# Moving three steps at the starts of two layers: a weight load to another queue, a pinned division, later denominators

## The chip, the cores and the metric

The kernel runs on one core of a Trainium2 chip. A core has a matrix engine (TensorE, PE in the profile), a vector engine (VectorE, DVE), an activation engine (ScalarE, ACT), a general engine (GpSimd, POOL) and a sync engine (SyncE, SP). They run side by side and wait for each other through semaphores. In this kernel SP and POOL also issue most of the transfers between the chip's main memory and the on-chip memory; each of them issues in its own order. The metric is the time of one execution on the device, in microseconds (us).

## The reference

Four graph layers in sequence on 3327 nodes with 512 features. Every layer adds its result to its input and normalises each row:

```python
x = _layernorm(x + _L0_gnn_ref(x, adj, L0_gnn_W, L0_gnn_a), axis=-1)
x = _layernorm(x + _L1_gnn_ref(x, adj, L1_gnn_W_nb, L1_gnn_b_nb, L1_gnn_W_line, L1_gnn_b_line, 64), axis=-1)
x = _layernorm(x + _L2_gnn_ref(x, adj, L2_gnn_W, L2_gnn_a), axis=-1)
x = _layernorm(x + _L3_gnn_ref(x, adj, L3_gnn_W, L3_gnn_a), axis=-1)
```

Layers 0, 2 and 3 are attention over the neighbours, with 8, 8 and 4 heads; layers 2 and 3 apply ELU to the result. For one head of layer 3:

```python
e = si[:, :, None] + sj[:, None, :]
e = jnp.where(e > 0, e, ALPHA * e)
e = jnp.where(adj[None, :, :] > 0, e, NEG_INF)
attn = jax.nn.softmax(e, axis=-1)
h_prime = jnp.einsum('hij,hjd->hid', attn, h)
```

Layer 1 takes the mean of a node's first 64 neighbours (in index order) and two linear maps:

```python
keep = Ab & (jnp.cumsum(Ab.astype(jnp.int32), axis=1) <= neibor_num)
nb_mean = (keep.astype(X.dtype) @ X) / jnp.maximum(cnt, 1.0)
xj = leaky_relu(nb_mean @ W_nb.T + b_nb)
xi = leaky_relu(X @ W_line.T + b_line)
return xi + jnp.where(cnt > 0, xj, 0)
```

## The kernel before

The rows are cut into NT = 26 tiles of 128 rows, and these into two halves of HALF = 13 tiles. Tiles are counted from 0, so the "fifth tile" is tile 4.

An attention layer first projects all tiles, then forms the attention of each half in four strips of columns. What a strip yields is still to be divided by the softmax's denominator: numerators go through tiles called hb to a tensor hd in main memory, and the denominators are collected on chip in rec. For the last strip of the second half they take a way round: they are summed on DVE to a tile red (line 505), stored to a tensor dd (line 507) and loaded back, rearranged, by 16 small transfers to a tile pes (place, lines 510 to 520). finish_sums (lines 525 to 538) then turns pes into the reciprocals in rec, by four DVE operations (lines 532 and 536) and a reciprocal (line 538). In layers 0 and 2 both steps of the last strip are put in a list, self.late, and done by the layer that follows. Only tiles 13 to 25 need them.

The next layer starts by finishing the rows of the last one, in pairs of tiles. finish_steps (line 165) gives a list of steps: load brings the numerators (h from hd, line 126) and the layer's input (xr, line 126); divide(s) multiplies the tile by rec on DVE (line 181) and, for ELU, has ACT take the exponential to a tile e (line 186); add(s) adds the input on DVE (line 197, or lines 194 and 195 with ELU); norm_rows takes the statistics (lines 152 and 153), a square root on ACT (line 154), a reciprocal and a product on DVE (lines 155 and 158), and normalises on ACT (line 161). The exponential and the square root lie in different tables of ACT, and the table is loaded again whenever it changes.

PE's instructions run in the order in which the program emits them. The instructions of the other engines and queues are put in order by a scheduler, except that keep_in_program_order pins an instruction behind everything that was emitted before it on its engine.

Layer 1 is sage (line 686). It loads two weights wn and wl (lines 716 and 717, through load_w, 1 MB each) and a bias on POOL. Then a loop goes over pairs of tiles. For each tile PE transposes it (pt, line 724), ACT copies it back (xT, line 726), and one tile later PE applies both weights (pz, line 732; pi, line 735) and DVE and ACT finish (lines 736 to 746). During the first tile of a pair the next pair is finished. At t0 = 4 the loop takes place from the late list, at t0 = 8 finish_sums.

Layer 3 starts in third (line 892). The loop is alike: PE transposes a tile (pt, line 261), ACT copies it (xT, line 262), DVE sums it (line 263), and one tile later PE projects it (pw, line 271), ACT and DVE scale the result (lines 272 to 277: dc, rc, qc, vt) and SP stores vt. load_group issues the loads of a pair three pairs ahead, with ten h buffers; the rest of a pair's steps is emitted during the first tile of the pair before it. After tile 14's transpose and tile 13's projection the loop prepares the attention of the first half (prepare, lines 298 to 322; PE's part is pr, line 312, and ACT's copy line 314). In finish_steps the argument pinned pins the exponential of a pair's first tile on ACT; it is set for the pair that begins with tile 2. Here too place is called at t0 = 4 and finish_sums at t0 = 8.

Of the kernel before, what the change touches and what calls it, by code (L numbers as in the profile page):

```python
# [32 lines left out]
def kernel(  # L33
# [10 lines left out]
    nc = tc.nc  # L44
# [90 lines left out]
    def load_w(pool, src, name, eng=None):  # L135
        t = pool.tile([P, FC, src.shape[1]], F32, name=name)
        (eng or nc.scalar).dma_start(out=t, in_=src.rearrange("(c p) m -> p c m", p=P))
        return t
# [26 lines left out]
    def finish_steps(pool, xin, layer, t0, n, hbufs=6, eng=nc.sync, xbufs=None, xpool=None, ebufs=None, pinned=False):  # L165
        H, D = layer.H, layer.D
        ys, xs, steps = [], [], []

        def load():
            for t in range(t0, t0 + n):  # L170
                h = pool.tile([P, F], F32, name="h", bufs=hbufs)
                load_tile(h, hd, t, eng)
                ys.append(h)
                xr = xpool.tile([P, F], F32, name="xr", tag="hb") if xpool else \
                    pool.tile([P, F], F32, name="xr", bufs=xbufs)
                load_tile(xr, xin, t, nc.gpsimd)
                xs.append(xr)

        def divide(s):
            h = ys[s]  # L180
            nc.vector.tensor_tensor(h.rearrange("p (h d) -> p h d", h=H), h.rearrange("p (h d) -> p h d", h=H),
                                    rec[:, t0 + s, :H].rearrange("p (h e) -> p h e", e=1).to_broadcast([P, H, D]),
                                    op=ALU.mult)
            if layer.elu:
                e = pool.tile([P, F], F32, name="e", bufs=ebufs)
                ins = nc.scalar.activation(e, h, AF.Exp)
                if pinned and s == 0:
                    tc.keep_in_program_order(ins)
                xs.append(e)

        def add(s):
            h, xr = ys[s], xs[s]
            if layer.elu:
                nc.vector.scalar_tensor_tensor(xr, xs[n + s], 1.0, xr, op0=ALU.min, op1=ALU.add)
                nc.vector.scalar_tensor_tensor(h, h, 0.0, xr, op0=ALU.max, op1=ALU.add)
            else:
                nc.vector.tensor_tensor(h, h, xr, op=ALU.add)

        steps.append(load)
        for s in range(n):  # L200
            steps += [lambda s=s: divide(s), lambda s=s: add(s)]
        steps.append(lambda: norm_rows(pool, ys, t0))
        return ys, steps

    def finish(*a):
        ys, steps = finish_steps(*a)
        for f in steps:
            f()
        return ys
# [476 lines left out]
    def sage(first, first_pool, xin, prev, nxt, wsrc, dst):  # L686
# [3 lines left out]
        with tc.tile_pool(name="sg_z", bufs=1, reuse_waits="tile") as zp, \  # L690
# [17 lines left out]
            def zs(t, c):  # L708
                return zs_[t // HALF][:, t % HALF, c, :]

            zd = dram.tile([NP, F], BF, name="zd")
            with tc.tile_pool(name="sa_w", bufs=1, reuse_waits="tile") as wp, \
                    tc.tile_pool(name="sa", bufs=2, reuse_waits="tile") as fp, \
                    tc.tile_pool(name="sa_t", bufs=2, reuse_waits="tile") as sp, \
                    tc.tile_pool(name="sa_ps", bufs=2, space=PSUM, reuse_waits="tile") as ps:
                wn = load_w(wp, wnT, "wn", nc.gpsimd)
                wl = load_w(wp, wlT, "wl", nc.gpsimd)
                blb = wp.tile([P, F], F32, name="blb")
                nc.gpsimd.dma_start(out=blb, in_=bl.to_broadcast([P, F]))

                def step1(xt):
                    pt = ps.tile([P, FC, P], F32, name="pt")
                    for c in range(FC):
                        nc.tensor.transpose(pt[:, c, :], xt[:, c * P:(c + 1) * P], ident)  # L724
                    xT = sp.tile([P, FC, P], F32, name="xT")
                    nc.scalar.copy(xT, pt)  # L726
                    return xT

                def step2(xt, xT, t):
                    pz = ps.tile([P, F], F32, name="pz")  # L730
                    for c in range(FC):
                        nc.tensor.matmul(pz, xT[:, c, :], wn[:, c, :], start=c == 0, stop=c == FC - 1)  # L732
                    pi = ps.tile([P, F], F32, name="pi")
                    for c in range(FC):
                        nc.tensor.matmul(pi, xT[:, c, :], wl[:, c, :], start=c == 0, stop=c == FC - 1)  # L735
                    nc.scalar.copy(zs(t, 0), pz)
                    r1 = sp.tile([P, F], F32, name="r1")
                    nc.vector.tensor_tensor(r1, pz, zs(t, 0), op=ALU.subtract)
                    nc.scalar.copy(zs(t, 1), r1)
                    z3 = sp.tile([P, F], BF, name="z3")  # L740
                    nc.vector.tensor_tensor(z3, r1, zs(t, 1), op=ALU.subtract)
                    nc.sync.dma_start(out=zd[t * P:(t + 1) * P, :], in_=z3)
                    xi = sp.tile([P, F], F32, name="xi")
                    nc.vector.tensor_tensor(xi, pi, blb, op=ALU.add)
                    nc.vector.scalar_tensor_tensor(xi, xi, 0.01, xi, op0=ALU.mult, op1=ALU.max)
                    nc.vector.tensor_tensor(xi, xi, xt, op=ALU.add)
                    nc.sync.dma_start(out=xid[t * P:(t + 1) * P, :], in_=xi)


                cr = fp.tile([NT, P], BF, name="cr", bufs=1)  # L750
                nc.sync.dma_start(out=cr, in_=ctd[NT:NT + 1, :].rearrange("o (t p) -> (o t) p", p=P))
                cnt = zp.tile([P, 3, NT], F32, name="cnt")
                pend = None
                ahead = first
                for t0 in range(0, NT, 2):
                    ys = ahead
                    if t0 in (4, 8):
                        prev.late.pop(0)(fp)
                    if t0 == 8:
                        cf = fp.tile([NT, P], F32, name="cf", bufs=1)  # L760
                        nc.scalar.copy(cf, cr)
                        pt = ps.tile([P, FC, P], F32, name="pt")
                        cb = pt[:, 0, :NT]
                        nc.tensor.transpose(cb, cf, ident[:NT, :NT])
                        nc.vector.tensor_scalar(cnt[:, 0, :], cb, NEIGHBOURS, 1.0, op0=ALU.min, op1=ALU.max)
                        nc.vector.reciprocal(cnt[:, 1, :], cnt[:, 0, :])
                        nc.vector.tensor_scalar(cnt[:, 2, :], cb, 0.0, None, op0=ALU.is_gt)
                    for s, y in enumerate(ys):
                        xT = step1(y)
                        if s == 0 and t0 + 2 < NT:  # L770
                            ahead = finish(fp, xin, prev, t0 + 2, 2, 6, nc.sync if t0 else nc.gpsimd)
                        if pend:
                            step2(*pend)
                        pend = (y, xT, t0 + s)
                step2(*pend)
            first_pool.close()

            with tc.tile_pool(name="sb_w", bufs=1, reuse_waits="tile") as wp, \
# [69 lines left out]
                for b in range(len(blocks)):  # L848
                    t0, i0 = blocks[b]
# [42 lines left out]
    def third(first):  # L892
        with tc.tile_pool(name="col3", bufs=1) as cp, tc.tile_pool(name="at_r3", bufs=2, reuse_waits="tile") as rp:
# [3 lines left out]
            with tc.tile_pool(name="p_w", bufs=1, reuse_waits="tile") as wp, \  # L897
# [13 lines left out]
                def load_group(t0):  # L911
                    if t0 < NT:
                        groups.append(finish_steps(fp, x2, L2, t0, 2, 10, nc.gpsimd if t0 < 4 else nc.sync, 6,
                                                    pinned=t0 == 2))
                        groups[-1][1].pop(0)()

                load_group(2)
# [2 lines left out]
                load_group(4)  # L920
                for t0 in range(0, NT, 2):
                    ys = ahead
                    if t0 in (4, 8):
                        L2.late.pop(0)(fp)
                    load_group(t0 + 6)
                    for s, y in enumerate(ys):
                        t = t0 + s
                        store_tile(x3, y, t, nc.sync)
                        xT = L3.project1(pp, ps, y, t)
                        if s == 0 and groups:  # L930
                            ahead, steps = groups.pop(0)
                            for f in steps:
                                f()
                        if pend:
                            L3.project2(pp, bank, wsb, *pend)
                        pend = (xT, t)
                        if t == HALF + 1:
                            L3.prepare(pp, 0)
                            L3.first_rows = L3.rows(rp, 0, 0)
                            L3.cut(pp, 0)  # L940
# [284 lines left out]
```

## Time and profile before

| | |
|---|---|
| time, median of 3 runs | 3389.97 us (3388.6 to 3393.65) |
| the profiled execution's own time | 3389.15 us |
| its span in the trace | 3387.4 us |
| mean granted clock of PE | 0.985 |
| PE busy | 3251.2 us, 96% of the span |
| DVE busy | 2687.5 us, 79% |
| ACT busy | 2354.6 us, 70% |
| POOL busy | 239.8 us, 7% |
| layer 1 starts (first transposes of sage) | near 958 us of the span |
| layer 3 starts (first transposes of third) | near 2556 us of the span |

Times inside the trace are us from the start of the span. A row of the timeline has the start, the length, the engine, the line, the operation, the tile written <- the tiles read with their shapes, the number of instructions in a row, and in brackets the idle time of the engine before it and what ended it. A row of the chain of waits has the start, the length and what the time went to: an engine with tile and line, a transfer (DMA), or "issue", time in which nothing that the profile shows was waited for. A row of the windows has the stretch, its length, the busy time of PE, PE's weight loads, DVE, ACT and POOL with their number of instructions, PE's granted clock, the busy share of the DMA engines, and GB/s.

### The profile page before, as it was taken

Reading aid. Unit: us, or ns where it says so; the run is one execution under the profiler, and the core shown is the slowest. Engines: PE = TensorE matmul, PEld = TensorE weight load, DVE = VectorE, ACT = ScalarE, POOL = GpSimd, SP = SyncE. Lnnn points to the kernel's source line nnn. Section 1 sums busy time; section 2 is a strip of 40 time slices with the busy share of each in tenths; the row PEclk is TensorE's granted clock in tenths of the full one; section 3 lists DMA queues with packets and bytes.
Section 4 is the critical chain, followed back from the end, with each engine's and each line's share of the span. In section 5 each row is a group of like instructions: output and inputs, shape, how many; then the busy total and the mean of one; then the engine's idle time right before and its main releaser. Section 6 shows DMA issues by size and latency. Waiting matters only on the chain.

```text
span 3387.4 us, 47182 instructions
## 1 busy us (share of the span) xinstructions
PE 3251.2 (96%) x18476; PEld 1626.4 (48%) x18476; DVE 2687.5 (79%) x2619; ACT 2354.6 (70%) x2143; POOL 239.8 (7%) x389
## 2 busy tenths in 40 slices
PE   8899999999979999999989999999998999999997
PEld 7634344444434445545544444444446754455453
DVE  5799999999967544444449999999998766668887
ACT  2398998999953333333338999999997655558986
POOL 3100000000010011111110000000002000010110
PEclk9999999999999999999999999999998999999998
DMA  9644111110143343333320111111117411122211
GB/s 368 222 124 127 49 49 38 55 49 28 44 123 125 122 117 84 91 85 87 80 77 20 47 48 50 51 48 47 35 31 241 152 41 42 41 51 80 94 42 49
DMA packets 288014, 284.29 MB, mean 84 GB/s; under 512 B 107492, under 2 KB 223534, under 8 KB 287791
## 3 DMA queue, kind: packets, MB, share of 16 engines
q1 hardware_dynamic: 254063, 170.62, 16.6%
q0 software_dynamic: 28208, 102.96, 9.5%
q10 hardware_dynamic: 5520, 7.69, 0.7%
q8 instruction: 146, 2.39, 0.3%
q14 instruction: 77, 0.63, 0.1%
HBM read 212.01 MB, written 69.17 MB: 83 GB/s over the span
## 4 chain that ended last, share of the span: by engine, by line
PE 85%; DVE 5%; DMA 4%; ACT 3%; issue 2%; SPq 0%; ACTq 0%; DVEq 0%; POOL 0%; POOLq 0%
PE po L428 52%; PE acc L859 12%; PE pd L380 7%; PE pw L271 5%; DVE t L405 3%; PE pz L732 3%; DMA raw<-in_adjT_dram 3%; PE pi L735 3%; ACT y L408 1%; PE pt L456 1%; PE pk L819 1%; DMA h<-hd 0%; PE pa L1108 0%; PE pt L724 0%; PE pct L664 0%
## 5 line engine op out<-in xcount | busy, mean ns | idle before, releaser
L405 DVE SCALAR_TENSOR_TENSOR t<-rb,qc,mask 128x1664 f32<-128x1664 f32 x1040 | 1960.3, 1954 | 169.4 <-PE po L428 147.3
L408 ACT ACTIVATE y<-t,bi,sc 128x1664 fp8e4<-128x1664 f32 x1040 | 1769.5, 1766 | 310.4 <-PE pd L380 292.7
L428 PE MATMUL po<-t,vj 128*64 128x448 f32 (+3 forms) x8320 | 1909.6, 521 | 22.1 <-DVE t L405 19.6
L428 PEld LDWEIGHTS po<-t,vj 128*64 128x64 f32 (+1 forms) x8320 | 838.9, 148 | 970.6 <-issue 704.0
L859 PE MATMUL acc<-zs,kt 128*128 128x512 bf16 x1352 | 401.1, 380 | 0.0
L271 PE MATMUL pw<-wsb,xT 128*128 128x264 f32 (+1 forms) x1248 | 302.2, 397 | 15.2 <-DVE vt L277 12.0
L859 PEld LDWEIGHTS <-kt 128*128 128x128 fp8e4 x2002 | 196.1, 98 | 242.1 <-issue 7.7
L811 ACT CAST pk<-cy 128x512 f32<-128x512 bf16 x169 | 99.0, 588 | 277.4 <-DVE kt L823 266.3
L271 PEld LDWEIGHTS pw<-wsb,xT 128*128 128x128 f32 x1248 | 241.1, 197 | 60.7 <-ACT xT L262 10.8
L380 PE MATMUL pd<-y,sden 128*32 128x448 fp8e4 (+1 forms) x4160 | 259.5, 342 | 10.4 <-ACT y L408 10.4
L859 PE MATMUL acc<-zl,kt 128*128 128x512 bf16 x650 | 246.5, 379 | 0.0
L380 PEld LDWEIGHTS <-sden 128*32 128x32 bf16 x4160 | 117.5, 96 | 162.5 <-issue 139.8
L823 DVE SCALAR_TENSOR_TENSOR kt<-pk,mask 128x512 fp8e4<-128x512 f32 x169 | 116.1, 688 | 94.0 <-PE pk L819 94.0
L277 DVE TENSOR_TENSOR vt<-pw,dc 128x256 f32<-128x256 f32 x156 | 59.0, 418 | 148.2 <-ACT dc L272 143.7
L359 POOL DMA_DIRECT2D rb<-r x40 | 21.3, 532 | 1670.4 <-DVE t L405 1652.2
L275 ACT COPY rc<-pw 128x8 f32<-128x8 f32 (+1 forms) x78 | 12.6, 162 | 156.6 <-PE pw L271 154.1
L831 DVE SCALAR_TENSOR_TENSOR y<-acc,cnt,bnb 128x512 f32<-128x512 f32 x26 | 19.5, 751 | 97.7 <-PE acc L859 90.3
L732 PE MATMUL pz<-wn,xT 128*128 128x512 f32 x208 | 94.9, 600 | 1.7 <-ACT xT L726 1.7
L700 POOL DMA_DIRECT2D cy<-ctd x91 | 67.9, 746 | 385.1 <-ACT pk L811 312.6
L735 PE MATMUL pi<-wl,xT 128*128 128x512 f32 x208 | 93.5, 592 | 0.0
L634 DVE TENSOR_SCALAR mask<-raw 128x832 fp8e4<-128x832 int32 (+2 forms) x90 | 54.8, 614 | 38.9 <-DMA raw<-in_adjT_dram 38.5
L154 ACT ACT_TABLE_LOAD x45 | 57.7, 1283 | 37.0 <-DVE mv L153 36.4
(187 smaller groups left out, 1699.3 us busy)
## 6 DMA issues: line engine op xcount, KB each, us to landing
vj<-v SPq DMA_DIRECT2D x312, 128.0 KB
rb<-r POOLq DMA_DIRECT2D x40, 832.0 KB, 4.8
raw<-in_adjT_dram SPq DMA_DIRECT2D x67, 416.0 KB
cy<-ctd POOLq DMA_DIRECT2D x78, 256.0 KB, 4.0
h<-hd SPq DMA_DIRECT2D x61, 256.0 KB
v<-vt SPq DMA_DIRECT2D x50, 256.0 KB
hd<-hb SPq DMA_DIRECT2D x48, 256.0 KB
xr<-x POOLq DMA_DIRECT2D x45, 256.0 KB, 3.1
```

Source lines behind the costliest of these rows:

```text
L271: nc.tensor.matmul(pw[e][:, :FW + H], xT[:, c, :], wsb[:, c, e, :], start=c == 0, stop=c == FC - 1)
L277: nc.vector.tensor_tensor(vt[:, hs, :], pw[e][:, :FW].rearrange("p (h d) -> p h d", d=D), self.dc[:, t, hs].rearrange("p (h e) -> p h e", e=1)
L380: nc.tensor.matmul(pd[c][32 * kk:32 * kk + 32, :w_], lhsT, rhs, start=(kk, c) not in seen, skip_group_check=final is not None, stop=last a ...
L405: nc.vector.scalar_tensor_tensor(t, rb[k], self.qc[:, j, h:h + 1], mask[:, j, i0:i0 + IW], op0=ALU.max, op1=ALU.mult)
L408: nc.scalar.activation(y, t, AF.Sigmoid, bias=self.bi[:, j, h:h + 1], scale=self.sc[:, j, h:h + 1], saturate=False)
L428: nc.tensor.matmul(po[c][k * D:(k + 1) * D, :z - a_], vj[:, j % 2, k * D:(k + 1) * D], ts[k][:, a_:z], start=j == 0, stop=j == NT - 1)
L700: nc.gpsimd.dma_start(out=cy[:, :n, :], in_=ctd[t:t + n, b * GW:(b + 1) * GW] .rearrange("(o t) i -> o t i", o=1).to_broadcast([P, n, GW]))
L732: nc.tensor.matmul(pz, xT[:, c, :], wn[:, c, :], start=c == 0, stop=c == FC - 1)
L735: nc.tensor.matmul(pi, xT[:, c, :], wl[:, c, :], start=c == 0, stop=c == FC - 1)
L811: nc.scalar.copy(pks[k % 2], carry[b, t // 4 * 4][:, t % 4:t % 4 + 2, :])
L823: nc.vector.scalar_tensor_tensor(kt, pk, NEIGHBOURS, mask[:, t:t + 2, i0:i0 + GW], op0=ALU.is_le, op1=ALU.mult, saturate=False)
L859: nc.tensor.matmul(acc, kts[t][:, s * P:(s + 1) * P], zs(t, c) if c < 2 else zl[:, t, :], start=t == 0 and c == 0, stop=t == NT - 1 and c ...
```

## The change

Three things are changed. In layer 1 the weight wn is loaded through SP's queue instead of POOL's. In finish_steps the division of a pair's first tile can be pinned too: for pinned equal to 2 both division and exponential are pinned, for True the division alone. third passes 2 for the pair of tiles 2 and 3, whose exponential was pinned before, and True for the pair of tiles 4 and 5; so tile 4's division now stands behind what was emitted before it on DVE, among this the norms of tiles 2 and 3. And the two late steps, place and finish_sums, are taken at t0 = 6 and 10 instead of 4 and 8, in sage and in third.

```diff
         def divide(s):
             h = ys[s]
-            nc.vector.tensor_tensor(h.rearrange("p (h d) -> p h d", h=H), h.rearrange("p (h d) -> p h d", h=H),
+            ins = nc.vector.tensor_tensor(h.rearrange("p (h d) -> p h d", h=H), h.rearrange("p (h d) -> p h d", h=H),
                                     rec[:, t0 + s, :H].rearrange("p (h e) -> p h e", e=1).to_broadcast([P, H, D]),
                                     op=ALU.mult)
+            if pinned and s == 0:
+                tc.keep_in_program_order(ins)
             if layer.elu:
                 e = pool.tile([P, F], F32, name="e", bufs=ebufs)
                 ins = nc.scalar.activation(e, h, AF.Exp)
-                if pinned and s == 0:
+                if pinned == 2 and s == 0:
                     tc.keep_in_program_order(ins)
...
-                wn = load_w(wp, wnT, "wn", nc.gpsimd)
+                wn = load_w(wp, wnT, "wn", nc.sync)
...
-                    if t0 in (4, 8):
+                    if t0 in (6, 10):
                         prev.late.pop(0)(fp)
...
                         groups.append(finish_steps(fp, x2, L2, t0, 2, 10, nc.gpsimd if t0 < 4 else nc.sync, 6,
-                                                    pinned=t0 == 2))
+                                                    pinned=(t0 == 2) * 2 or t0 == 4))
...
-                    if t0 in (4, 8):
+                    if t0 in (6, 10):
                         L2.late.pop(0)(fp)
```

## The prediction

> **What bounds the kernel now.** I read the page's chain of waits first, then TensorE (PE) by windows, then the timelines of PE, VectorE (DVE) and ScalarE (ACT) at the two places where the diff acts: the start of layer 1 and the start of layer 3. The chain is
>
> ```profile
> PE 85%; DVE 5%; DMA 4%; ACT 3%; issue 2%; SPq 0%; ACTq 0%; DVEq 0%; POOL 0%; POOLq 0%
> ```
>
> so the time moves only where PE stands still. At the start of layer 1:
>
> ```profile
> 966.53 3.60 PE L735 MATMUL pi<-wl,xT 128*128 128x512 f32 x8
> 983.97 1.11 PE L724 MATMUL pt<-ident,h 128*128 128x128 f32 x4 [13.84 <-ACT h L161]
> ```
>
> In brackets is the idle time before the row and what ended it: 13.84 us until tile 2 was normed. The chain inside it is the denominators' store and loads:
>
> ```profile
> 961.81 7.10 DMA dd<-red
> ...
> 971.52 4.67 DMA pes<-dd
> 976.21 3.86 DMA pes<-dd
> ```
>
> At the start of layer 3, PE by timeline, then one row by windows:
>
> ```profile
> 2573.51 1.12 PE L261 MATMUL pt<-ident,h 128*128 128x128 f32 x4 [8.46 <-ACT h L161]
> 2574.42 5.42 PE L271 MATMUL pw<-wsb,xT 128*128 128x260 f32 x16
> 2579.68 0.60 PE L261 MATMUL pt<-ident,h 128*128 128x128 f32 x4
> 2580.12 3.67 PE L271 MATMUL pw<-wsb,xT 128*128 128x260 f32 x16
> 2583.63 0.60 PE L261 MATMUL pt<-ident,h 128*128 128x128 f32 x4
> ...
> 2574.00:2600.00 26.00, 26.00 (x122) 22.20 (x122) 23.46 (x56) 22.29 (x43) 3.76 (x7) 0.92 0.84 275
> ```
>
> A row pt is the transpose that opens a tile, so tile 2 opens at 2573.51, tile 3 at 2579.68 and tile 4 at 2583.63; a tile costs PE 3.95 us. Tile 4 came without a wait and PE was full from 2574 to 2600 (the columns after the length are PE, weight loads, DVE, ACT). DVE beside it, and the late denominators:
>
> ```profile
> 2562.96 1.40 DVE L181 TENSOR_TENSOR h<-h,rec 128x512 f32<-128x512 f32 x2 [4.52 <-DMA h<-hd]
> ...
> 2572.46 0.15 DVE L158 SCALAR_TENSOR_TENSOR rs<-mv,rs 128x2 f32<-128x2 f32 x1
> ...
> 2602.73 0.20 DVE L532 SCALAR_TENSOR_TENSOR rec<-pes,rec 128x52 f32<-128x52 f32 x1
> ...
> 2604.15 0.80 DVE L538 RECIPROCAL rec<-rec 128x104 f32<-128x104 f32 x1
> 2604.99 1.89 DVE L181 TENSOR_TENSOR h<-h,rec 128x512 f32<-128x512 f32 x3
> ```
>
> DVE stood 4.52 us behind tile 4's division, whose load had not landed. The denominators finish at 2604.95. PE opened tile 12, the first pair that needs them (tiles 12 and 13 are normed together), at 2616.71, and ACT's norm of that pair started at 2615.69: it came just in time.
>
> **What the Trainium skill says.** "TensorE: Matmul & The Clock Gate", What's actually happening: after about 3.4 us without work PE falls to half clock and needs about as long to recover. The trace agrees: after the 8.46 us gap a tile's pw took 5.42 us instead of 3.67, and after a gap of 3.64 us 5.36. I price a cold restart at 1.7 us. "ScalarE: Activation LUTs", What ACT_TABLE_LOAD costs: 1283 ns for each load, whatever the set; the page's row has 1283 too. "DMA: Bandwidth & Descriptors", Issuing engines are not separate DMA queues: all queues share 16 engines, and issuing from another engine saves only issue time. Here the queues show it: four h loads on SP at 2553.36 needed 9.6 us (the chain's DMA h<-hd) while GpSimd's (POOL's) loads were under way.
>
> **Part 1: the weight wn on SP.** The same 1 MB is moved. POOL issued it at 950.35 (0.75 us) and then stood 6.88 us on ACT's L408 before the next issue, wl; that wait stays, so POOL's later loads gain nothing. On SP the issue comes before the hb and dd stores (959.60, 961.81), nine us earlier than they can go, so they are not pushed back: 0. What else moves here comes from the later place of the late loads: SP's order now has only three pes loads ahead of the h loads of tiles 4 to 7 where six stood, so the load for tile 4, issued at 972.89, goes about 2 us earlier and the wait of 2.25 us on it at 977.21 shrinks. Against that, on POOL one 256 KB cy load moves ahead of tile 2/3's second h and xr (about 0.75 us), and xr now waits for the last of the four hb stores (0.7 to 1.5 us); and a further division and add (0.6 each) fall before tile 2's L155 and L158. I come out at L158 within 0.2 us of before: boundary 0, bounds -1.5 and +2.5. The finishing of the sums (L532 to L538) goes to about 1047, with PE needing tile 12 at about 1066 and a chain of 14 us at most: 0. From there to layer 3 the order of instructions is the same and PE is full.
>
> **Part 2: tile 4's division pinned in layer 3.** Laid out by the changed order with the durations of the trace: DVE does tile 2's division, then those of tiles 5, 6, 7 (loads land to about 2564.9), so it still waits for the same burst of loads; the wait is not taken away, only its instruction. Then L194, L195, L152 and L153 of tiles 2 and 3, the divisions of tiles 8 to 11, L155, L158 at about 2572.5: where it was. Tile 2 opens at 2573.5: gain 0. In before, tile 4's exp, L194, L195 and statistics ran in this gap. Now its division waits for L158 and for L263 of tile 2 (ACT copies xT first): start 2575.9. Then division 0.7, table load 1.28, exp 0.63 (2578.5), L194 x2, L195 x2, L152 x2 at 0.6 (2582.2), L153, the square root 0.29 (2583.1), L155 behind L277, L263 and two L194 (2584.9), L195, L158 (2585.7), ACT's norm 0.80: 2586.5. PE was free at 2583.2: +3.4 us of idle time. Whether it restarts cold is open (3.4 against the 3.4 to 3.6 seen): 0 or 1.7. I take 1.7, so +5.1 at tile 5. Bounds: -2.5 (if L194 of tiles 2 and 3 does not stand behind the loads) and +6.
>
> **Part 3: late denominators in layer 3.** 16 pes issues of about 0.55 us stay on SP; they start at 2566.0 as before, waiting for dd, and are not needed before 2600. What counts is L532, pinned behind what was emitted before it: in before behind vt of tile 6, now behind vt of tile 8, that is two PE tiles, 7.9 us, later. After pw of tile 8 PE has only two tiles of work (7.9 us) before it opens tile 12. From that point the chain is L277 0.75, L532 to L536 1.42, L538 0.80, L181 0.69, exp 0.63, L194, L195, L152 2.07, L153 0.18, table and root 1.57, L155, L158 0.33, norm 0.80: 9.2 us at least. In before 13.98 us passed from L532 to tile 12's opening, as DVE (19.19 of 20 us busy there) also had other tiles' work. With that work in the changed order I get 13.2: +5.3 us of idle time, and 1.4 to 1.7 for the cold restart; together with part 2 PE is 10.3 late at tile 13. Bounds: 1.3 (9.2 less 7.9) and 6.9.
>
> Not all of it stays. Before, PE lost 1.30 us to xT at 2618.61, and at 2634.75 3.64 us in the first half's preparation (L312 waiting for ACT's L314) and 1.7 us for the restart. When PE comes later to these, ACT and DVE are ahead: I get 2.9 us off in that stage, net +7.4 at the last pw of the stage, after which PE is full (42.72 of 43.00 us before) and carries it to the end. Sum: 0 + 7.4, taken as +7.
>
> Base: the profiled execution took 3389.15 us (span 3387.4), and 3396 follows; the median of the runs is 3389.97, 0.8 higher, so I say 3397.
>
> **The rivals.**
> - Two stalls as above: 3397 (3393 to 3402). For it: ACT's norm of tile 12 had no slack, and tile 4's division goes later in the changed order.
> - One of the stalls is swallowed: tile 4 restarts warm and the preparation's 3.64 + 1.7 us and the 1.30 us absorb most of the second, net +3: 3393 (3390 to 3396). Against: the bubble is smaller than the sum of both.
> - Faster: the wait at the head of DVE goes. Place: the 4.52 us before tile 4's division; if tiles 2 and 3 norm ahead of the loads, tile 2 opens up to 2.5 us sooner, layer 1's start gives up to 1.5, and the 5.3 us of the preparation's bubble are partly recovered: about -5, 3385. It decides from the point where L194 of tile 2 runs before 2563. Against: the divisions of tiles 5 to 7 stand ahead of it in the changed order and wait for the same burst.
> - Two stalls, and layer 1's start loses too: the cy load and the last hb store delay xr, +2.5: 3400.
> - That the change does nothing is excluded by the order; that the pin doesn't remove the wait it is put against is the first case.
>
> **How the numbers follow.** What a measurement of this kernel tells from no change is 0.2%, 6.8 us. Chances: two stalls 0.48 (0.38 beyond 6.8 us, 0.10 within), one swallowed 0.20 (0.02, 0.18), faster 0.20 (0.17 faster by more, 0.03 within), with layer 1 0.12 (0.10, 0.02). Faster 0.17, same 0.33, slower 0.50. Predicted 3397. The range takes the bottom of the one-stall case and half of the faster one, and the top of the two stalls: 3386 to 3402; the likeliest's own is 3393 to 3402.
>
> **What would show it.** Tile 2 of layer 3 opens at 2573 to 2574; PE idles 3 to 4 us before tile 4 and 4 to 6 before tile 12, each ended by ACT h L161, with a pw of about 5.4 us after each; L532 comes after 2612; in layer 1 PE restarts within 2 us of 983.97. I'm wrong if tile 4 opens without a wait, or tile 12's norm keeps up, or tile 2 opens before 2571.

## The result and the profile after

The changed kernel is slower: 3394.89 us against 3389.72 us, medians of 20 runs each, ratio 1.0014 (95% interval 1.0008 to 1.002). That is about 4.7 us (0.0014 x 3390), with an interval of 2.7 to 6.8 us. The profiled execution has a span of 3393.7 us, 6.3 more than before.

In the changed kernel every line after 183 has a number two higher: before's L261 is L263, L271 is L273, L312 is L314, L532 is L534, L724 is L726. (Of the experiments' kernels, those with the pin, 2, 5, 7 to 10 and 12, have the same numbers; 1, 3, 4, 6 and 11 have before's.) Layer 3's projection stage first, PE by timeline (start, length, engine, line, operation, tiles, and in brackets the idle time before and what ended it):

```profile
2576.87 1.12 PE L263 MATMUL pt<-ident,h 128*128 128x128 f32 x4 [9.72 <-ACT h L161]
2577.78 5.87 PE L273 MATMUL pw<-wsb,xT 128*128 128x260 f32 x16
...
2589.86 0.66 PE L263 MATMUL pt<-ident,h 128*128 128x128 f32 x4 [2.26 <-ACT h L161]
2590.35 3.67 PE L273 MATMUL pw<-wsb,xT 128*128 128x260 f32 x16
...
2626.80 1.12 PE L263 MATMUL pt<-ident,h 128*128 128x128 f32 x4 [5.05 <-ACT h L161]
2627.70 4.81 PE L273 MATMUL pw<-wsb,xT 128*128 128x260 f32 x16
...
2641.03 1.03 PE L314 MATMUL pr<-ident,rc 128*4 128x128 f32 x8 [0.62 <-ACT rc L309]
2643.19 0.75 PE L314 MATMUL pr<-ident,rc 128*4 128x128 f32 x5 [1.13 <-ACT rr L316]
```

The three pt rows with a wait are tiles 2, 4 and 12. Tile 4, which came without a wait before, now costs 2.26 us; tile 12 costs 5.05 us and a slower pw (4.81 against 3.67). The preparation (the pr rows), on the other hand, waits less. Before, the same place read:

```profile
2630.08 1.04 PE L312 MATMUL pr<-ident,rc 128*4 128x128 f32 x8
2634.75 0.75 PE L312 MATMUL pr<-ident,rc 128*4 128x128 f32 x5 [3.64 <-ACT rr L314]
...
2635.77 5.36 PE L271 MATMUL pw<-wsb,xT 128*128 128x260 f32 x16
```

So 3.64 us of idle time and a cold tile (5.36 us) have become 1.75 us and a warm one (the next pw, at 2644.21, takes 3.67 us). DVE of the changed kernel, by timeline, at the two new waits:

```profile
2566.77 2.12 DVE L181 TENSOR_TENSOR h<-h,rec 128x512 f32<-128x512 f32 x3 [3.19 <-DMA h<-hd]
...
2575.81 0.16 DVE L158 SCALAR_TENSOR_TENSOR rs<-mv,rs 128x2 f32<-128x2 f32 x1
2578.64 0.69 DVE L265 TENSOR_REDUCE xsum<-xT 128x4 f32<-128x512 f32 x1 [2.67 <-ACT xT L264]
2579.24 0.68 DVE L181 TENSOR_TENSOR h<-h,rec 128x512 f32<-128x512 f32 x1
2581.95 1.29 DVE L196 SCALAR_TENSOR_TENSOR xr<-e,xr 128x512 f32<-128x512 f32 x2 [2.02 <-ACT e L188]
...
2614.15 0.75 DVE L279 TENSOR_TENSOR vt<-pw,dc 128x256 f32<-128x256 f32 x2 [0.17 <-ACT rc L277]
2614.82 0.20 DVE L534 SCALAR_TENSOR_TENSOR rec<-pes,rec 128x52 f32<-128x52 f32 x1
...
2616.21 0.80 DVE L540 RECIPROCAL rec<-rec 128x104 f32<-128x104 f32 x1
2617.05 0.69 DVE L181 TENSOR_TENSOR h<-h,rec 128x512 f32<-128x512 f32 x1
...
2625.74 0.15 DVE L158 SCALAR_TENSOR_TENSOR rs<-mv,rs 128x2 f32<-128x2 f32 x1
```

Tile 4's division is the L181 at 2579.24. It stands behind L265 of tile 2, and that behind tile 2's opening on PE. DVE idles 2.67 us before it, and 2.02 us after it while ACT forms the exponential. The wait for the burst of loads (3.19 us at 2566.77) is still there, only with other tiles' divisions at its head. The finishing of the sums starts at 2614.82, behind a vt, and the norm it leads to is ready for ACT at 2625.89.

What this does to DVE shows in the windows from the pw after tile 2's transpose to the pw after tile 14's. The columns are the stretch, its length, and the busy time of PE, weight loads, DVE, ACT and POOL. First before, then after:

```profile
2574.42:2626.57 52.15, 49.87 (x242) 42.55 (x241) 47.87 (x112) 41.34 (x89) 5.91 (x11) 0.97 0.78 258
```

```profile
2577.78:2636.73 58.95, 51.63 (x241) 43.76 (x241) 50.69 (x118) 45.26 (x92) 7.52 (x14) 0.93 0.70 227
```

The stretch is 6.8 us longer. DVE's idle time in it goes from 4.3 us (52.15 - 47.87) to 8.3 us. This stage has two engines nearly full: 96% of the stretch on PE and 92% on DVE before.

Layer 1's start, PE by timeline:

```profile
985.57 1.11 PE L726 MATMUL pt<-ident,h 128*128 128x128 f32 x4 [14.46 <-ACT h L161]
986.48 6.15 PE L734 MATMUL pz<-wn,xT 128*128 128x512 f32 x8
```

The gap is 14.46 us where it was 13.84, and the first pz took 6.15 us where it took 4.83.

To leave out what happened earlier in the span, I use two stage lengths below. Each begins with the start of the row pd<-mask,sm, which PE does near the end of the attention layer before; "the last pd" means this row. For layer 1: from the last pd of layer 0 (952.41 before, 953.40 after) to the start of the last pz (1161.33 and 1164.25): 208.9 and 210.9 us. For layer 3's projection: from the last pd of layer 2 (2547.97 and 2552.09) to the start of the last row of pw<-wsb,xT (2676.92 and 2683.85), which holds the pw of tiles 24 and 25: 129.0 and 131.8 us.

### The profile page after: what moved, and what is told of

It is laid out like the page before. It is cut to its first block, busy times and chain, and to the rows that moved or that the text cites. A ratio compares the mean times of both kernels' runs of the same rounds, so it can differ in the third digit from the quotient of the medians.

```text
span 3393.7 us, 47128 instructions
## 1 busy us (share of the span) xinstructions
PE 3251.7 (96%) x18424; PEld 1629.2 (48%) x18476; DVE 2686.7 (79%) x2619; ACT 2357.5 (69%) x2145; POOL 238.6 (7%) x388
## 4 chain that ended last, share of the span: by engine, by line
PE 85%; DVE 5%; DMA 4%; ACT 3%; issue 2%; SPq 0%; ACTq 0%; DVEq 0%; POOL 0%; POOLq 0%
PE po L430 51%; PE acc L861 12%; PE pd L382 7%; PE pw L273 6%; PE pz L734 3%; DVE t L407 3%; PE pi L737 3%; DMA raw<-in_adjT_dram 2%; ACT y L410 2%; PE pk L821 1%; PE pt L458 1%; DMA h<-hd 1%; DMA asb<-in_a_dram 0%; PE pt L263 0%; PE pa L1110 0%
## 5 line engine op out<-in xcount | busy, mean ns | idle before, releaser
L861 PE MATMUL acc<-zs,kt 128*128 128x512 bf16 x1312 | 392.7, 380 | 2.1
L273 PE MATMUL pw<-wsb,xT 128*128 128x264 f32 (+1 forms) x1248 | 303.6, 399 | 11.6 <-DVE vt L279 11.0
L273 PEld LDWEIGHTS pw<-wsb,xT 128*128 128x128 f32 x1248 | 242.9, 198 | 56.5 <-issue 10.5
```

Source lines behind the costliest of these rows:

```text
L273: nc.tensor.matmul(pw[e][:, :FW + H], xT[:, c, :], wsb[:, c, e, :], start=c == 0, stop=c == FC - 1)
L861: nc.tensor.matmul(acc, kts[t][:, s * P:(s + 1) * P], zs(t, c) if c < 2 else zl[:, t, :], start=t == 0 and c == 0, stop=t == NT - 1 and c ...
```

## The experiments

Each ratio is against runs of the kernel before on the same chip; one thousandth is 3.4 us. Stage lengths are from the one profiled execution of each kernel; where layer 3's program is the same they still differ, by 1.2 us among before, 1, 4 and 6 and by 2.4 us between the change and 5.

| kernel | ratio (95% interval) | layer 1 stage | layer 3 stage |
|---|---|---|---|
| before | 1 | 208.9 | 129.0 |
| the change | 1.0014 (1.0008 to 1.002) | 210.9 | 131.8 |
| 1: wn on SP | 1.0000 (0.9992 to 1.0009) | 210.0 | 128.9 |
| 2: pin | 0.9996 (0.9988 to 1.0004) | 208.7 | 129.3 |
| 3: late steps of layer 3 | 1.0000 (0.9992 to 1.0008) | 208.7 | 130.0 |
| 4: late steps of layer 1 | 1.0003 (0.9994 to 1.0011) | 210.7 | 129.0 |
| 5: pin, late steps of layer 3 | 1.0015 (1.0008 to 1.0021) | 208.5 | 134.1 |
| 6: wn, late steps of layer 1 | 1.0000 (0.9992 to 1.0008) | 210.7 | 127.7 |
| 7: pin, pair of tile 4 earlier | 1.0018 (1.0011 to 1.0024) | 210.5 | 133.0 |
| 8: pins, pairs of tiles 4 and 6 earlier | 1.0026 (1.0015 to 1.0037) | 209.0 | 136.1 |
| 9: pin, place at 6, finish_sums at 8 | 1.0004 (0.9996 to 1.0012) | 209.0 | 130.3 |
| 10: the change, finish_sums not pinned | 1.0006 (0.9998 to 1.0014) | 211.3 | 130.3 |
| 11: preparation one tile later | 0.9984 (0.9977 to 0.999) | 208.8 | 125.1 |
| 12: pin and preparation later | 0.9998 (0.9989 to 1.0006) | 208.9 | 127.9 |

### The parts alone (1 to 4)

The diff's edits, one at a time, on the kernel before.

```diff
-                wn = load_w(wp, wnT, "wn", nc.gpsimd)
+                wn = load_w(wp, wnT, "wn", nc.sync)
```

> Only wn moved to SP's queue. Theory A (layer 1 loses through the later place of the late loads): layer 1's first stage is as before, PE's restart within 0.7 us after the same dd store, total 0 (-2 to +2) us. Rival B (the weight on SP delays the numerators' stores): the restart after the dd store is about 1 to 2 us later, total +2 us.

```diff
+            if pinned and s == 0:
+                tc.keep_in_program_order(ins)
...
-                if pinned and s == 0:
+                if pinned == 2 and s == 0:
...
-                                                    pinned=t0 == 2))
+                                                    pinned=(t0 == 2) * 2 or t0 == 4))
```

> Only tile 4's division pinned. Theory A: PE waits 2 to 4 us for ACT L161 before tile 4 of layer 3, without a cold restart; by the end of the projection a part is given back in the preparation's bubble: +1 to +3 us. Rival C (the pin frees DVE and tile 2 opens earlier, or the bubble swallows all): 0 to -2 us.

```diff
-                    if t0 in (4, 8):
+                    if t0 in (6, 10):
                         L2.late.pop(0)(fp)
```

> Only layer 3's late steps moved to t0 = 6 and 10. Theory A: PE waits 4 to 6 us for ACT L161 before tile 12, and L312's wait of 3.6 us shrinks to under 2: net +1 to +4 us at the end of the projection. Rival C (all of it swallowed by the preparation's bubble): 0 us with the wait at tile 12 still there. If tile 4's pin is what makes tile 12 late: no wait at tile 12.

```diff
-                    if t0 in (4, 8):
+                    if t0 in (6, 10):
                         prev.late.pop(0)(fp)
```

> Only layer 1's late steps moved to t0 = 6 and 10. Theory A: PE's restart in layer 1 comes 0.5 to 2 us later than in the kernel before, counted from the dd store, total +0.5 to +2 us. Rival B (the weight on SP does it): restart as before, total 0 us.

None of the four moved the time by as much as its measurement tells, about 3 us. In layer 1, PE restarted 22.16 us after the dd store before, 22.27 us in 1 and 22.62 in 4: theory A's place for both, at the lower edge for 4. In layer 3 the waits are there. PE by timeline with the pin alone (tile 4, and the preparation):

```profile
2586.88 0.88 PE L263 MATMUL pt<-ident,h 128*128 128x128 f32 x4 [3.41 <-ACT h L161]
2587.56 5.17 PE L273 MATMUL pw<-wsb,xT 128*128 128x260 f32 x16
...
2635.54 1.03 PE L314 MATMUL pr<-ident,rc 128*4 128x128 f32 x8 [0.72 <-ACT rc L277]
2637.79 0.75 PE L314 MATMUL pr<-ident,rc 128*4 128x128 f32 x5 [1.21 <-ACT rr L316]
```

and with layer 3's late steps alone (tile 12, and the preparation):

```profile
2618.22 1.11 PE L261 MATMUL pt<-ident,h 128*128 128x128 f32 x4 [3.82 <-ACT h L161]
...
2633.31 1.03 PE L312 MATMUL pr<-ident,rc 128*4 128x128 f32 x8 [1.37 <-ACT rc L307]
2635.29 1.23 PE L312 MATMUL pr<-ident,rc 128*4 128x128 f32 x5 [0.94 <-ACT rr L314]
```

Each loses 3.4 to 3.8 us at its tile, and more for the cold pw, and each meets a preparation that waits 1.9 to 2.3 us instead of 3.64. I had expected +1 to +3 us for the pin and +1 to +4 for the late steps. The times favour the rival "swallowed" for both, but their intervals reach up to +1.4 and +2.7 us, and the stages are 0.4 and 1.1 us longer. For the pin I had also said "without a cold restart", and it was cold.

### The parts in pairs (5 and 6)

The edits of layer 3 together, and those of layer 1 together; the diffs are those above.

> Both edits of layer 3, none of layer 1. Theory A (each edit opens idle gaps on DVE in a stage where DVE has almost none to spare, and the preparation's bubble can swallow one of them, not both): from the last pd of layer 2 to the last pw about +2.8 us against the kernel before, more than the sum of the two alone (+0.4 and +1.1); time +2 to +4 us. Rival D (the parts add up): +1.5 us. Rival E (layer 3 does nothing, the loss of the whole change is layer 1's): 0.

> Both edits of layer 1, none of layer 3. Theory A: from the last pd of layer 0 to the last pz +1 to +2 us, of it about 0.5 a later restart and the rest a longer cold first pz (about 6.1 us where the kernel before has 4.83); time +1 to +2 us. Rival E (layer 1 alone makes the whole loss): +4 us or more. Rival F (the longer cold start is chance): first pz 4.8 us, time 0.

Layer 3's pair makes a loss as large as the whole change's: 1.0015, some 5.1 us, and 134.1 us of stage against 129.0 (the change's own profile has 131.8). Alone its parts came to 0.9996 and 1.0000, so they don't add up; rivals D and E fall, though the loss was also larger than theory A's +4. Its PE has both waits, as the change has:

```profile
2586.94 0.66 PE L263 MATMUL pt<-ident,h 128*128 128x128 f32 x4 [2.45 <-ACT h L161]
...
2623.88 1.12 PE L263 MATMUL pt<-ident,h 128*128 128x128 f32 x4 [5.06 <-ACT h L161]
```

Layer 1's pair measured 1.0000, which excludes that layer 1 alone makes the loss and leaves +1 to +2 us and zero both open. In the trace, layer 1's stage was 1.8 us longer in 4 and in 6, but also 1.6 us longer in 7, whose layer 1 is that of before. The other seven kernels with before's layer 1 have 208.5 to 209.0, so 7 is the exception.

### Moving the pin's place (7 and 8)

In 7 both divisions of the pair of tiles 4 and 5 are pinned, and the pair's steps are emitted at the end of the first pair's loop pass instead of after tile 2's transpose. In 8 the same for tiles 4 to 7.

```diff
-                        if s == 0 and groups:
-                            ahead, steps = groups.pop(0)
-                            for f in steps:
-                                f()
+                        if s == 0 and groups and t0 not in early:
+                            nexts.append(groups[0][0])
+                            for f in groups.pop(0)[1]:
+                                f()
...
+                        if t0 == 0 and s == 1:
+                            for _ in early:
+                                nexts.append(groups[0][0])
+                                for f in groups.pop(0)[1]:
+                                    f()
```

Here early is (2,) in 7 and (2, 4) in 8, and the loop takes its pair from nexts.

> As the pin alone, but both divisions of tiles 4 and 5 are pinned and that pair's steps are emitted one tile earlier, before tile 2's transpose, so that tile 4's division need not wait for L263 of tile 2; late steps at t0 = 4 and 8. Theory A: tile 4 opens without a wait or with under 1 us, tile 2 as early as with the pin alone (1.5 us sooner than before): stage -1 to -3 us. If the pin's place behind L263 isn't what makes tile 4 late, its wait stays at 2 to 3.5 us.

> The divisions of tiles 4 to 7 are all pinned behind the norm of tiles 2 and 3 and both pairs' steps are emitted before tile 2's transpose, so nothing on DVE waits for the loads of tiles 4 to 7 ahead of L194 of tile 2; late steps at t0 = 4 and 8. Theory A (the hole of 3 to 4.5 us on DVE before these loads is what the stage is short of): tile 2 opens 2.5 to 4 us sooner and most is kept: time -2 to -4 us. Rival (the preparation's bubble takes it back, or tiles 6 and 12 come late): 0.

In 7 tile 4's wait went, as theory A said: its pin behind L265 of tile 2 is what makes tile 4 late. But the time is 6 us up, where theory A had the stage 1 to 3 us shorter. PE, then DVE by timeline:

```profile
2585.67 0.66 PE L263 MATMUL pt<-ident,h 128*128 128x128 f32 x4 [0.20 <-ACT h L161]
...
2637.32 1.35 PE L314 MATMUL pr<-ident,rc 128*4 128x128 f32 x8 [4.31 <-ACT rc L309]
```

```profile
2626.18 0.69 DVE L181 TENSOR_TENSOR h<-h,rec 128x512 f32<-128x512 f32 x1 [1.40 <-DMA h<-hd]
2628.10 0.69 DVE L181 TENSOR_TENSOR h<-h,rec 128x512 f32<-128x512 f32 x1 [1.22 <-DMA h<-hd]
```

In the new order two divisions wait for their loads just ahead of what the preparation needs, and PE stands 4.31 us at its first step. Up to tile 13's opening PE was on time (74.2 us after the last pd, as before), so the loss comes behind it; that these two waits make it is read from the order and was not tested. In 8 tile 2 opened 3.0 us sooner in the stage, as expected, but the time rose by some 9 us (1.0026), which neither theory nor rival had. DVE:

```profile
2562.81 1.29 DVE L196 SCALAR_TENSOR_TENSOR xr<-e,xr 128x512 f32<-128x512 f32 x2 [1.43 <-ACT e L188]
...
2582.14 1.50 DVE L181 TENSOR_TENSOR h<-h,rec 128x512 f32<-128x512 f32 x2 [4.97 <-DMA h<-hd]
```

The hole before the adds of tiles 2 and 3 is gone; a hole of 4.97 us has opened behind, where two divisions stand whose loads had not landed. My forecast of -2 to -4 us was wrong: I had reckoned with one hole, and the rest of the order changed with it.

### The late sums (9 and 10)

9 is the pin with layer 3's late steps at t0 = 6 and 8. 10 is the whole change, with the pinned operations of finish_sums (two of the four, L534) not pinned for layer 2's denominators:

```diff
-                        if HS > 1:
+                        if HS > 1 and self.li != 2:
                             tc.keep_in_program_order(ins)
```

> The pin of tile 4 with place at t0 = 6 but finish_sums back at t0 = 8 (layer 3 only; wn and layer 1 as before). Theory A (it is finish_sums behind vt of tile 8, not the later transfers, that starves tile 12): the 5 us wait before tile 12 shrinks to under 2 us, time within 2 us of the kernel before. Rival G (the later pes loads push other loads): wait and loss stay, +4 us or more.

> The whole change, but the four operations of finish_sums of layer 2's denominators are not pinned on DVE, so they no longer stand behind vt of tile 8 though they are emitted at t0 = 10. Theory A: no wait over 2 us before tile 12; time +0 to +2 us against the kernel before, 3 to 5 us less than the change. Rival H (the wait at tile 12 comes from the later start of tile 4 alone): the wait stays near 5 us and the time at +5.

The wait before tile 12 was 2.46 us in 9 (theory A had said under 2) and 1.00 in 10, against 5.06 and 5.05 in their counterparts 5 and the change. Times: 1.0004 and 1.0006, near the kernel before; the intervals overlap those of the counterparts a little, so it is the waits that separate them. In 10 the sums wait for something else, on DVE:

```profile
2603.27 0.21 DVE L534 SCALAR_TENSOR_TENSOR rec<-pes,rec 128x52 f32<-128x52 f32 x1 [2.90 <-DMA pes<-dd]
```

Free to go early, they met the later pes loads. So for the greater part it is the pinned place of finish_sums, behind vt of tile 8, that makes tile 12 late. The later transfers may have a share: 9 differs from 2 only in taking place at t0 = 6 instead of 4, and has 2.46 us before tile 12 where 2 has 0.68; no run takes this apart.

### The sink, and a faster version (11 and 12)

```diff
-                        if t == HALF + 1:
+                        if t == HALF + 2:
                             L3.prepare(pp, 0)
```

11 has this edit alone on the kernel before; 12 has it with the pin.

> The kernel before with layer 3's first-half preparation emitted one tile later (after tile 15's transpose, not 14's), nothing else. Theory A (the idle 3.6 us and the cold tile at L312 are PE standing behind ACT and DVE; work put ahead of it fills them): the wait at L312 falls to under 2 us, the next pw is 3.67 and not 5.36, time -3 to -5 us. Rival (DVE sets the stage's end in any case): wait moves, time 0.

> Tile 4's division pinned and the preparation emitted one tile later; late steps at t0 = 4 and 8, layer 1 as before. With the preparation at its old place the pin alone cost nothing (0.9996). Theory A (the pin does cost about 2.6 us up to tile 13, and the preparation's idle time gave it back): with that idle time filled, the pin costs 2 to 4 us against the later preparation alone, so about 0 to -3.5 us against the kernel before. Rival J (the pin costs nothing in itself): the gain of the later preparation stays whole, -5 us or more.

11 is 5.4 us faster than before (0.9984; 3.9 us by the stages) and beats both kernels. PE at the preparation:

```profile
2637.26 1.04 PE L312 MATMUL pr<-ident,rc 128*4 128x128 f32 x8
2638.52 0.75 PE L312 MATMUL pr<-ident,rc 128*4 128x128 f32 x5 [0.23 <-ACT rr L314]
...
2639.55 3.67 PE L271 MATMUL pw<-wsb,xT 128*128 128x260 f32 x16
```

The wait of 3.64 us is 0.23, the next pw warm. Now the pin, which cost nothing alone, costs 4.7 us (0.9998 against 0.9984, with intervals that just touch; 2.9 us by the stages), which is near theory A's 2 to 4 us, and rival J falls. But 12's profile doesn't show the cost on theory A's path. At tile 13's opening PE is only 0.5 us later than in 11, where theory A had 2.6: tile 2 opened 1.5 us sooner and tile 4 left PE warm. Most of the 2.9 us comes at the preparation, where PE waits again, and behind it:

```profile
2639.18 0.75 PE L314 MATMUL pr<-ident,rc 128*4 128x128 f32 x5 [1.79 <-ACT rr L316]
```

So 11 shows that the preparation's idle time can be won, and 12 that the pin isn't free once it is. That this idle time was the sink that hid a single new wait fits kernel 2, where PE was 2.7 us late at tile 13 and 0.4 at the last pw, but it isn't shown in full. From tile 13 to the last pw PE got back 2.3 us in 2, 1.2 in 3, 1.6 in 5 and 3.2 in the change; and of what 5 loses beyond 2 and 3 together, about half is there at tile 13 already (6.8 us late, against 2.7 and 2.3), ahead of the preparation. Why the two edits cost more together than alone stays open in part.

## Why the prediction came out as it did

The direction, and the two places on PE, were as forecast. The size was too large: +7 us against 4.7. By the prediction's own line of 6.8 us the measured change counts as the same time, to which it gave 0.33, and only 0.10 of that with two stalls. Of the steps:

| step | forecast | the change | kernel 5 |
|---|---|---|---|
| tile 2's opening | 0 | -0.8 | +0.1 |
| idle before tile 4 | 3.4 | 2.26 | 2.45 |
| cold restart there | 1.7 | 0 | 0 |
| idle before tile 12 | 5.3 | 5.05 | 5.06 |
| cold restart there | 1.4 to 1.7 | 1.1 | 1.0 |
| PE late at tile 13's opening | 10.3 | 6.0 | 6.8 |
| given back after that | 2.9 | 3.2 | 1.6 |
| late at the last pw | 7.4 | 2.8 | 5.2 |

The lateness is counted from the last pd of layer 2.

- Part 2, the pin. "gain 0" at tile 2 held within what the profiles scatter (24.0 to 25.9 us after the last pd with the pin, 24.9 to 25.9 without), and so did the reason, that the wait is not taken away but only its instruction. The chain behind the pin was laid out right: on paper tile 4 opens 13.0 us after tile 2 (2586.5 less 2573.5), and it took 12.98 to 13.00 us in all six kernels with the pin at this place (the change, 2, 5, 9, 10 and 12). Mis-sized was PE's own work in these 13 us. The pw after tile 2's transpose was cold and took 4.73 to 6.07 us in these kernels, and the wait at tile 4 was what it left, 3.41 to 2.06 us: the two add up to 8.1 us each time. With the 5.42 us of before that is 2.7 us, not 3.4; the forecast had PE free at 2583.2, where its own line has the pw end at 2583.79 (2580.12 + 3.67). The second mis-sized term is the cold restart behind tile 4: I took 1.7 of "0 or 1.7", and it was 0 in five of the six and 1.5 in kernel 2 (5.17 less 3.67), which had the longest gap.
- Part 3, the late sums. 5.3 us against 5.05, by the mechanism named: from the end of pw of tile 8 (2613.85) to tile 12's opening passed 12.95 us where 13.2 was forecast, with 7.9 us of work on PE in both. Kernels 9 and 10 take most of the wait away. The sum, 10.3 us late at tile 13, was 4.3 too high (and it is not the sum of the terms shown, 5.1, 5.3 and 1.4 to 1.7, which make 11.8 to 12.1). 2.9 of that had come in by tile 5, with part 2's terms: there PE was 5.1 us late on paper and 2.2 on the chip (2594.29 against 2588.01, less the 4.12 us by which the last pd came later). The other 1.4 lies between tiles 5 and 11: the kernel before takes 25.2 us there (2588.01 to 2613.20), the changed one 23.8 (2594.29 to 2618.07). 0.98 of it is a wait for xT at 2601.26 that the changed kernel doesn't have; the prediction names no such term.
- "Not all of it stays", 2.9 us: 3.2 and 1.6 us. The size was right for the change; that the preparation's idle time can be won is shown by 11. What I did not see is that the parts depend on each other: I gave a rival "one of the stalls is swallowed" a price of +3, and each stall alone measures 0 within 3 us.
- Part 1, layer 1. Boundary 0 with bounds of -1.5 and +2.5: its stage was 1.9 us longer in the profile, mostly a longer cold pz; no measurement of time resolves it. Kernel 1 shows no cost of wn's queue, within 3 us.
- The faster rival fell at the point given for it: L194 (L196) of tile 2 ran at 2568.80, behind the loads; less the 4.12 us this is 2564.7, and the point was 2563.
- Of the signs named, the wait at tile 12 and layer 1's restart were met. The wait at tile 4 was under its 3 to 4 us, the two pw behind the waits took 3.67 and 4.81 us and not 5.4, and L532 (L534) came at 2610.7 and tile 2 opened at 2572.75 when the 4.12 us are taken off, both sooner than said.

That the waits of kernel 5 are those of the change and its loss as large, with layer 1 untouched, shows that layer 3's two edits are enough for the 4.7 us. The change's own profile has 2.8 of them in layer 3 and 1.9 in layer 1; how much layer 1 adds stays open within about 2 us.

## What to carry to other kernels

- An edit that measures zero alone can cost together with another: two edits at 0.9996 and 1.0000 made 1.0015. Try the edits in pairs before calling a part free. And look for idle time further down that may hide a wait: filling it here (one tile's work put ahead of the preparation) won 5.4 us, more than any of the edits.
- A wait on PE is what PE's own work leaves of a chain elsewhere: here tile 4 opened 13.0 us after tile 2 in six kernels, and a slower pw in between only made the wait shorter.
- A pin moves an instruction behind everything emitted before it, here behind the next tile's own work on PE; ask what the last of these instructions waits for, not only which stall the pin is meant to avoid.
- Where two engines are both above 90% in a stage, count the idle time that an order leaves on the second; removing one hole can open others, as in kernel 8.

## What was unexpected of the hardware

Whether PE comes back at its slow pace after a short gap is not set by the gap's length alone. In kernel 9, by timeline:

```profile
2587.80 0.66 PE L263 MATMUL pt<-ident,h 128*128 128x128 f32 x4 [2.50 <-ACT h L161]
2588.29 3.67 PE L273 MATMUL pw<-wsb,xT 128*128 128x260 f32 x16
...
2623.30 0.66 PE L263 MATMUL pt<-ident,h 128*128 128x128 f32 x4 [2.46 <-ACT h L161]
2623.79 5.36 PE L273 MATMUL pw<-wsb,xT 128*128 128x260 f32 x16
```

A gap of 2.50 us left PE warm and one of 2.46 us made it cold; 2.82 us was warm in kernel 10. PE's granted clock was 1.00 in the first of these pw and 0.67 in the second. The Trainium skill, "TensorE: Matmul & The Clock Gate", says in What's actually happening that PE falls to its slow clock after an idle window of about 3.4 us, and that this window runs freely. Read as a threshold on one gap, the 3.4 us don't hold here, since 2.46 us were enough. That the outcome depends on where a gap falls in such a window would fit, but no run shows it. After the long gaps of layer 1 (13.6 to 15.5 us) the first pz took between 4.50 and 6.19 us, where a warm one takes 3.60.
